# A graph layer and a state-space layer on one core: GpSimd's softplus spread over four slots, ScalarE's moved by one, one of two comparisons moved to GpSimd, and the first image's last edges moved into the layer-1 loop

## The chip, the core and the metric

The kernel runs on one core of one Trainium2 chip. The metric is the device time of one execution in microseconds (us). "Before" has a median of 14244.15 us over three runs (14243.77 to 14252.39).

The engines are named as the profile names them: PE is TensorE (PEld are its weight loads), DVE is VectorE, ACT is ScalarE, POOL is GpSimd, SP is the engine whose queue issues most DMAs.

## The reference

The input x has 16 images of 96 channels by 64 by 64 pixels, float32. Two layers are computed one after the other.

Layer 0 works on windows of 8x8 pixels. A 1x1 convolution gives 64 nodes a window; each node finds its 9 nearest nodes; an edge function is computed for every neighbour and the largest value is kept:

```
nodes = window_partition(affine(conv1x1(x, fc1_w, fc1_b), fc1_s, fc1_t), 8)
idx   = knn_idx(nodes, 9)                      # top 9 of the normalized distances
feat  = concat(x_i, x_j - x_i)                 # x_j = nodes[idx]
h     = max over the 9 of gelu(affine(feat @ ew.T + eb, es, et))
x1    = affine(conv1x1(window_reverse(h), fc2_w, fc2_b), fc2_s, fc2_t) + x
```

Layer 1 treats an image as a sequence of 4096 positions and runs two state-space blocks over it, each with 192 channels and 16 states:

```
delta = softplus(dt @ dt_w + dt_b);   dA = exp(delta * A);   dBx = delta * B * xc
h[l]  = dA[l] * h[l-1] + dBx[l]       # for each channel and state, along the sequence
y     = (sum over states of h * C + D * xc) * silu(z);   seq = seq + y @ out_w
```

Then follow a fusing 1x1 convolution with a pooled term, a normalization over the whole batch, and the sum with layer 1's input.

## The kernel before

**Work units.** Layer 0 works by strips of 8 pixel rows, 512 positions, 8 strips an image. `nearest(b, q)` (lines 281 to 353) loads a strip, projects it, computes distances and picks the 8 neighbours of each node other than itself; `edges(b, q)` (355 to 475) does the rest of layer 0 in two halves (`hf`). In a half, the neighbours' numbers come back by DMA as 16-bit integers, broadcast to 64 partitions (`idb`, 362). Each is compared with the partition's own number to make a one-hot matrix: `Abs(idb - node)` (370) and `Relu(1 - that)` (371), two ACT operations on 64x1024 elements, once for each of two pairs of windows (`oh0`, `oh1`). Two products `pv` (380, 381) are copied to SBUF by ACT (`vu`, 383). For each pair, three products `t` of one-hot and `vu` (400, 403) go through Gelu on ACT (408); DVE reduces them by maximum in later slots (780). The node's own term (`sa`, `sb`, 426 and 438) is added in the second half.

Layer 1 works by items: one image, one block, one strip, 16 x 2 x 8 = 256 items. `norm(n)` (504 to 525) normalizes the strip; `prelude(n)` (527 to 611) projects it, applies the short convolution and SiLU, and computes softplus; `tail(n)` (657 to 685) projects back and, in the second block, computes `po` and the copy `o`.

**The main loop** (729 to 795) runs over 256 items x 8 slots, p = 0 to 7, each slot for two of the 16 states. In a slot DVE does three products `db` (635) and three scans `hb` (776), with other small work between them; PE broadcasts the next slot's B into `bt` (630) and folds an earlier slot's result over the states (`folded`: `ya`, `yb`, 646 and 648); ACT computes three exponentials `da` for a slot two ahead (624); POOL copies the state (791) and multiplies `hb` by C (792).

**The order is written out by hand** (`manual_schedule`, 699): every engine takes its instructions in the order in which the program emits them. Beside the scan, the steps of `norm`, `nearest`, `edges` and `tail` (the list `going`) and then those of `prelude` (the list `preps`) are advanced by one `yield` in each slot, between the first and the second scan. In PE's queue a slot m thus reads: `bt` for slot m+1, the steps' products, the fold of slot m-1. `bt` has one PSUM buffer; the steps' products share a ring of two (`mm`), so that a product waits until the last but one has been read. The exponentials of a slot are emitted in the middle of the slot for p = 0, 2, 4, ahead of the steps, and otherwise at its end; a step that yields `TABLE` holds the latter back for that slot.

For the prediction, these places matter. `prelude(n+2)` starts at p = 4 of item n. In item n, the steps of p = 0 to 3 therefore are:

- p = 0: `pc` and its square (515, 517) of `norm(n+2)`; first `pv` and `vu`; `po` and `o` (679, 681) in the second block; and ACT's four softplus passes of `prelude(n+1)` (589 to 594).
- p = 1: `pvar` (520) and the two ACT passes `rs` on it (522, 523); `ss` and its copy (306, 307) in even items; second `pv` and `vu`; POOL's first two softplus passes (596, 597).
- p = 2: `hn` on POOL (525); the first pair's three `t` and Gelus, with a table load ahead of the first; POOL's last two passes (599, 600).
- p = 3: the second pair's `t` and Gelus; 16 DMAs that double `ln` and `s1` into `delta` and `u` (607, 609).

`edges` starts at p = 5 of odd items with `idb`, the comparisons are at p = 6, and the second half starts one item later. `nearest` starts in the same slots; its product `pf` and copy `y` fall on p = 7 of odd items.

**Before the loop** come the loads of the constants, all issued on SP's queue (98 to 221); `nearest(0, 0)` alone; eight calls of `drain` (704), each with `nearest(0, q+1)` and `edges(0, q)` side by side (the last with `edges(0, 7)` alone); then `norm` and `prelude` of items 0 and 1. **After the loop** a normalization pass reads everything back, adds and writes the result (801 to 822).

Of the kernel before, what the change touches and what calls it, by code (L numbers as in the profile page):

```python
# [10 lines left out]
F32 = mybir.dt.float32  # L11
U16 = mybir.dt.uint16
AF = mybir.ActivationFunctionType
ALU = mybir.AluOpType
# [6 lines left out]
def tile_conv_knn_mamba(ctx: ExitStack, tc: tile.TileContext, w: dict, out: bass.AP):  # L21
# [29 lines left out]
    CB = 64  # L51
    NB3 = D // CB
# [4 lines left out]
    const = ctx.enter_context(tc.tile_pool(name="const", bufs=1))  # L57
# [5 lines left out]
    make_identity(nc, ident)  # L63
    cmat = const.tile([C, C], F32, name="cmat")
    nc.vector.tensor_scalar(cmat, ident[:C, :C], -1.0 / C, None, ALU.add)
    minus_node = const.tile([NN, 1], F32, name="minus_node")
    nc.gpsimd.iota(minus_node, pattern=[[0, 1]], base=0, channel_multiplier=-1, allow_small_or_imprecise_dtypes=True)
# [37 lines left out]
    def compact(name, src):  # L105

        t = const.tile([128, 2], F32, name=name)
        src = src.rearrange("(p o) -> p o", o=1)
        nc.sync.dma_start(out=t[:, 0:1], in_=src[:128])
        for h in range(2):  # L110
            nc.sync.dma_start(out=t[h * CB : (h + 1) * CB, 1:2], in_=src[128:])
        return t

    def rows(name, src, n):


        t = const.tile([128, 3, n], F32, name=name)
        nc.vector.memset(t, 0.0)
        nc.sync.dma_start(out=t[:, 0, :], in_=src[:128])
        for h in range(2):  # L120
            nc.sync.dma_start(out=t[h * CB : (h + 1) * CB, 1 + h, :], in_=src[128:])
        return t

    fc1T = load("fc1T", [C, C], w["L0_conv_fc1_w"])
# [39 lines left out]
    for i in range(NHN):  # L164
        t = const.tile([128, HALO + Q], F32, name=f"hn{i}")
# [3 lines left out]
    for i in range(2):  # L169
        t = const.tile([128, Q], F32, name=f"dbl{i}")  # L170
# [4 lines left out]
    with tc.tile_pool(name="setup", bufs=2) as sp, tc.tile_pool(name="setup_ps", bufs=2, space=PSUM) as spp:  # L175
        for i in range(NL):


            iw = sp.tile([C, 2 * D], F32, tag="iw", name=f"in_w{i}")
            nc.sync.dma_start(out=iw, in_=w["L1_conv_in_w"][i])  # L180
            g = sp.tile([C, 1], F32, tag="g", name=f"g{i}")
            nc.sync.dma_start(out=g, in_=w["L1_conv_ln_g"][i].rearrange("(p o) -> p o", o=1))
            lb = sp.tile([C, C + 1], F32, tag="lb", name=f"lb{i}")
            nc.vector.memset(lb, 0.0)
            nc.sync.dma_start(out=lb[:, C : C + 1], in_=w["L1_conv_ln_b"][i].rearrange("(p o) -> p o", o=1))
# [12 lines left out]
            cw = sp.tile([C + 1, NT, D], F32, tag="cw", name=f"cw{i}")  # L198
            nc.sync.dma_start(
                out=cw.rearrange("p k d -> p (k d)"),  # L200
                in_=w["L1_conv_conv_w"][i].rearrange("k d -> (k d)").unsqueeze(0).to_broadcast([C + 1, NT * D]),
            )
# [10 lines left out]
            nc.sync.dma_start(out=dw[:R], in_=w["L1_conv_dt_w"][i])  # L213
            nc.sync.dma_start(out=dw[R + 2 * NS : R + 2 * NS + 1], in_=w["L1_conv_dt_b"][i].rearrange("(o d) -> o d", o=1))
            dt_w.append(dw)
            an = const.tile([128, NB3, NPR], F32, name=f"a{i}")
            for k in range(NB3):
                for h in range(2):
                    nc.sync.dma_start(
                        out=an[h * CB : (h + 1) * CB, k, :],  # L220
                        in_=w["L1_conv_A_log"][i].rearrange("(k c) (n h) -> h k c n", c=CB, h=2)[h, k],
                    )
# [20 lines left out]
    pr = main.enter_context(tc.tile_pool(name="ring", bufs=2))  # L243
# [15 lines left out]
    def half(h):  # L259
        return slice(h * CB, (h + 1) * CB)  # L260
# [94 lines left out]
    def edges(b, q):  # L355

        nm = f"{b}_{q}"
        y = nodes_of.pop((b, q))
        idx_d = chosen_of.pop((b, q))
        for hf in range(2):  # L360
            idb = pr.tile([NN, NP, NN * KO], U16, tag="idb", name=f"idb_{nm}_{hf}", bufs=1)
            nc.sync.dma_start(
                out=idb.rearrange("j w n -> j (w n)"),
                in_=idx_d.rearrange("(s p) i k -> s (p i k)", s=2)[hf : hf + 1].to_broadcast([NN, NP * NN * KO]),
            )
            yield
            for p in range(2):

                ohj = ohs[p][0:NN].rearrange("j w i k -> j w (i k)")
                nc.scalar.activation(ohj, idb[:, 2 * p : 2 * p + 2, :], AF.Abs, bias=minus_node)  # L370
                nc.scalar.activation(ohj, ohj, AF.Relu, bias=1.0, scale=-1.0)
            yield
            yield
            vus = []
            for p in range(2):

# [150 lines left out]
    def prelude(n):  # L527
# [57 lines left out]
        for v, cols in ((va, slice(0, Q)), (vb, slice(Q, Q + QH))):  # L585
            nc.scalar.activation(e[:, cols], v, AF.Abs)
            nc.scalar.activation(rl[:, cols], v, AF.Relu)
        yield
        nc.scalar.activation(e, e, AF.Exp, scale=-1.0)
        s1 = pr.tile([128, Q + QH], F32, tag="s1", name=f"s1_{nm}", bufs=1)  # L590
        nc.scalar.activation(s1, e, AF.Identity, bias=1.0)
# [2 lines left out]
        nc.scalar.activation(s1, s1, AF.Identity, bias=neg1)  # L594
        yield
        nc.gpsimd.tensor_tensor(e, e, s1, ALU.subtract)  # L596
        nc.gpsimd.tensor_tensor(ln, ln, e, ALU.add)
        yield
        nc.gpsimd.tensor_tensor(ln, ln, rl, ALU.add)
        nc.gpsimd.tensor_tensor(s1, ln, xc, ALU.mult)  # L600
        yield
        pairs = []
        for what, src in (("delta", ln), ("u", s1)):
            t = pr.tile([128, NB3, Q], F32, tag=what, name=f"{what}_{nm}")
            for h in range(2):
                for k in range(2):
                    nc.sync.dma_start(out=t[half(h), k, :], in_=src[half(k), :Q])
                for k in range(2):
                    nc.sync.dma_start(out=t[half(h), 2, bass.ts(k, QH)], in_=src[half(k), Q:])
            pairs.append(t)  # L610
        made[n] = (xc, z, dbl, c_d, *pairs)

    def chosen(n, p):

# [86 lines left out]

    drain(nearest(0, 0))
    for q in range(NQ):
        drain(*([nearest(0, q + 1)] if q + 1 < NQ else []), edges(0, q))
    for n in range(2):
        drain(norm(n))
        drain(prelude(n))
# [141 lines left out]
```

## Time and profile before

| what | value |
|---|---|
| median of three runs | 14244.15 us |
| the profiled execution | 14254.24 us, span 14252.5 us |
| first `db` of the loop | 485.9 us after the start of the span |
| last scan of the loop | 13970.8 us |
| busy in the span | DVE 12875.6 us (90%), PE 12467.5 (87%), ACT 10536.6 (74%), POOL 10043.0 (70%) |
| busy from 4000 to 6000 us | DVE 1887.76, PE 1824.15, ACT 1547.43, POOL 1483.67 us of 2000 |
| granted PE clock over the span, from 4000 to 6000 us | 0.951, 0.97 |

The profile tells for each group of instructions its line in the kernel, the engine, the operation, the tiles as out<-in, the shapes and the count; behind the first bar the busy time in us and the mean of one in ns; behind the second bar how long the engine stood idle just before them, with what ended that. The timeline gives each instruction's start and duration in us, and in brackets the idle time before it and its releaser. PE's instructions are pipelined, so that their durations overlap; starts are read there.

### The profile page before, as it was taken

How to read it: one execution, taken by the hardware profiler on the slowest of the kernel's cores; microseconds unless marked ns; L12 is line 12 of the kernel's file. 1: busy time of each engine (PE TensorE's matmuls, PEld its weight loads, DVE VectorE, ACT ScalarE, POOL GpSimd, SP SyncE). 2: the span in 40 equal slices, each digit the busy share in tenths (PEclk: the TensorE clock that was granted, in tenths of full speed). 3: DMA queues.
4: the chain of work that ended last, by engine and by line, in shares of the span. 5: the costliest groups of instructions: out<-in, count | busy, mean ns of one | idle time of the engine just before them, and what ended most of it. 6: DMA issues, size and time to landing. Idle time of an engine off the chain costs nothing. (4 is left out here: it accounts for less than half of the span.)

```text
span 14252.5 us, 162557 instructions
## 1 busy us (share of the span) xinstructions
PE 12467.5 (87%) x47944; PEld 4659.7 (33%) x47944; DVE 12875.6 (90%) x16893; ACT 10536.6 (74%) x15157; POOL 10043.0 (70%) x6151
## 2 busy tenths in 40 slices
PE   5799999999999999999999999999999999999871
PEld 2233333333333333333333333333333333333320
DVE  2699999999999999999999999999999999999984
ACT  4577777777777777777777777777777777777652
POOL 0477777777777777777777777777777777777771
PEclk8899999999999999999999999999999999999985
DMA  1233333333333333233333333333333333333227
GB/s 25 57 85 86 80 85 84 84 82 81 87 83 81 86 84 84 80 85 84 86 81 84 86 81 82 84 86 85 81 86 83 84 81 83 87 84 81 78 76 226
DMA packets 887149, 1206.23 MB, mean 85 GB/s; under 512 B 282272, under 2 KB 413742, under 8 KB 877040
## 3 DMA queue, kind: packets, MB, share of 16 engines
q1 hardware_dynamic: 882672, 1170.66, 31.1%
q10 hardware_dynamic: 3584, 25.17, 0.4%
q8 instruction: 377, 6.18, 0.2%
q14 instruction: 516, 4.23, 0.1%
HBM read 706.82 MB, written 85.72 MB: 56 GB/s over the span
## 5 line engine op out<-in xcount | busy, mean ns | idle before, releaser
L792 POOL TENSOR_TENSOR hb<-hb,ct 128x1536 f32<-128x1536 f32 x2048 | 7068.3, 3452 | 608.4 <-DVE hb L776 233.2
L776 DVE TENSOR_TENSOR_SCAN hb<-da,state,db 128x512 f32<-128x512 f32 x5376 | 6808.9, 1270 | 0.0
L635 DVE TENSOR_TENSOR db<-u,bt 128x512 f32<-128x512 f32 x6144 | 3988.9, 679 | 827.1 <-PE bt L630 827.1
L624 ACT ACTIVATE da<-delta,a 128x512 f32<-128x512 f32 x6144 | 3903.5, 716 | 38.5 <-DVE hb L776 32.5
L646 PE MATMUL ya<-hb,fold 128*64 128x512 f32 x8192 | 2324.1, 647 | 410.9 <-POOL hb L792 409.4
L630 PE MATMUL bt<-dbl,bsel 128*128 128x512 f32 x4096 | 2351.0, 656 | 101.0 <-DVE db L635 85.8
L408 ACT ACTIVATE g<-t,eb,es 128x512 f32<-128x512 f32 x1536 | 1178.3, 776 | 1098.9 <-PE t L400 660.2
L791 POOL COPY state<-hb 128x3 f32<-128x3 f32 x1792 | 336.2, 188 | 2219.9 <-DVE hb L776 2162.6
L648 PE MATMUL yb<-hb,fold 128*64 128x256 f32 x8192 | 1292.7, 395 | 0.0
L554 ACT ACTIVATE xc<-pj,conv_b 128x512 f32<-128x512 f32 (+1 forms) x512 | 297.1, 580 | 1058.0 <-PE pj L547 791.0
L648 PEld LDWEIGHTS yb<-hb,fold 128*64 128x64 f32 x8192 | 617.8, 144 | 1281.8 <-issue 1281.6
L400 PE MATMUL t<-oh,vu 128*128 128x512 f32 x2048 | 992.7, 607 | 31.8 <-ACT g L408 19.0
L646 PEld LDWEIGHTS ya<-hb,fold 128*64 128x64 f32 x8192 | 491.5, 142 | 1448.1 <-POOL hb L792 675.6
L630 PEld LDWEIGHTS bt<-dbl,bsel 128*128 128x128 f32 x4096 | 639.1, 193 | 959.9 <-issue 501.9
L542 PE MATMUL pj<-hn,conv_in 128*128 128x512 f32 x2048 | 929.1, 596 | 9.2 <-POOL hn L525 9.2
L776 DVE TENSOR_TENSOR_SCAN hb<-da,db 128x512 f32<-128x512 f32 x768 | 924.6, 1210 | 2.3 <-ACT da L624 2.3
L596 POOL TENSOR_TENSOR e<-e,s 128x768 f32<-128x768 f32 x256 | 464.9, 1816 | 626.3 <-ACT s L594 593.4
L403 PE MATMUL t<-oh,vu 128*64 128x512 f32 x2048 | 604.5, 671 | 341.0 <-ACT g L408 337.4
L380 PE MATMUL pv<-ewT,y 96*64 96x192 f32 x2048 | 475.4, 358 | 257.9 <-ACT rs L522 247.5
L370 ACT ACTIVATE oh<-idb,minus_node 64x1024 f32<-64x1024 uint16 x512 | 581.1, 1135 | 71.8 <-DMA idb<-idxd 71.7
L780 DVE TENSOR_REDUCE hqa<-g 128x64 f32<-128x512 f32 x960 | 633.3, 660 | 0.0
L400 PEld LDWEIGHTS t<-oh,vu 128*128 128x128 f32 x2048 | 394.5, 195 | 555.6 <-issue 440.5
(164 smaller groups left out, 16884.9 us busy)
## 6 DMA issues: line engine op xcount, KB each, us to landing
ct<-cd SPq DMA_DIRECT2D x4096, 128.0 KB
delta<-ln SPq DMA_DIRECT2D x1024, 128.0 KB
u<-s SPq DMA_DIRECT2D x1024, 128.0 KB
idb<-idxd SPq DMA_DIRECT2D x256, 256.0 KB
delta<-ln SPq DMA_DIRECT2D x1024, 64.0 KB
u<-s SPq DMA_DIRECT2D x1024, 64.0 KB
x<-in_x SPq DMA_DIRECT2D x128, 192.0 KB
rn<-r4d SPq DMA_DIRECT2D x128, 192.0 KB
```

The costliest lines, as they stand in the source:

```text
L400: nc.tensor.matmul(t, lhsT=vus[p][:, part, :128], rhs=ohw[part], start=True, stop=True)
L403: nc.tensor.matmul(t[half(h)], lhsT=vus[p][:, h, 128:], rhs=ohw[h], start=True, stop=True)
L408: nc.scalar.activation(g, t, AF.Gelu, bias=e_b[:, j : j + 1], scale=e_s[:, j : j + 1])
L542: nc.tensor.matmul(ps, lhsT=wt[:, t, :128], rhs=hn[:, off : off + Q], start=(t == 0), stop=(t == taps - 1))
L624: nc.scalar.activation(da, delta[:, c, :], AF.Exp, scale=a_neg[i][:, c, p : p + 1])
L630: nc.tensor.matmul(bt, lhsT=bsel[:, p, :], rhs=made[n][2], start=True, stop=True)
L635: nc.vector.tensor_tensor(db, made[n][5][:, c, :], bt, ALU.mult)
L646: nc.tensor.matmul(y[0][half(h)], lhsT=fold, rhs=hb[:, h, :], start=False, stop=(p == NPR - 1))
L648: nc.tensor.matmul(y[1][half(h)], lhsT=fold, rhs=hb[:, 2, bass.ts(h, QH)], start=False, stop=(p == NPR - 1))
L776: nc.vector.tensor_tensor_scan(hb[:, c, :], das[c], dbs[c], state[:, p, c : c + 1] if k else 0.0, ALU.mult, ALU.add)
L780: between.popleft()()
L792: nc.gpsimd.tensor_tensor(hb, hb, ct.unsqueeze(1).to_broadcast([128, NB3, Q]), ALU.mult)
```

## The change

1. Softplus: ACT's four passes are emitted one slot later (p = 1 instead of p = 0), after the steps in `going`, so behind the two passes `rs` and the copies of that slot. POOL's four passes stand at p = 2, 3, 4 and 5, one in each, instead of two at p = 1 and two at p = 2. The eight DMAs to `delta` follow at p = 5, the eight to `u` at p = 6, instead of all at p = 3.
2. Comparisons: for the second pair ACT does the same two passes at p = 6; for the first pair POOL does one `is_equal` with the partition's number at p = 7.
3. The first image: `drain` runs `edges(0, 0)` to `edges(0, 5)` only. `edges(0, 6)` is advanced by three steps before the loop and goes on in it; `edges(0, 7)` starts at item 1. The later strips start where they did.
4. Constants: the loads in `compact` and `rows`, and those of the block's weights, are issued on ACT's queue instead of SP's.

```diff
@@ edges
-            for p in range(2):
-
+            for p in (1, 0):
                 ohj = ohs[p][0:NN].rearrange("j w i k -> j w (i k)")
-                nc.scalar.activation(ohj, idb[:, 2 * p : 2 * p + 2, :], AF.Abs, bias=minus_node)
-                nc.scalar.activation(ohj, ohj, AF.Relu, bias=1.0, scale=-1.0)
-            yield
-            yield
+                numbers = idb[:, 2 * p : 2 * p + 2, :]
+                if p == 0:
+                    nc.gpsimd.tensor_scalar(ohj, numbers, node, None, ALU.is_equal)
+                else:
+                    nc.scalar.activation(ohj, numbers, AF.Abs, bias=minus_node)
+                    nc.scalar.activation(ohj, ohj, AF.Relu, bias=1.0, scale=-1.0)
+                yield
@@ prelude
             nc.scalar.activation(rl[:, cols], v, AF.Relu)
         yield
+        yield
         nc.scalar.activation(e, e, AF.Exp, scale=-1.0)
...
         nc.gpsimd.tensor_tensor(e, e, s1, ALU.subtract)
+        yield
         nc.gpsimd.tensor_tensor(ln, ln, e, ALU.add)
         yield
         nc.gpsimd.tensor_tensor(ln, ln, rl, ALU.add)
+        yield
+        delta = pr.tile([128, NB3, Q], F32, tag="delta", name=f"delta_{nm}")
+        doubled(delta, ln)
+        u = pr.tile([128, NB3, Q], F32, tag="u", name=f"u_{nm}")
         nc.gpsimd.tensor_tensor(s1, ln, xc, ALU.mult)
-        yield
...
+        made[n] = (xc, z, dbl, c_d, delta, u)
+        yield
+        doubled(u, s1)
+
+    def doubled(t, src):
+
+        for h in range(2):
+            for k in range(2):
+                nc.sync.dma_start(out=t[half(h), k, :], in_=src[half(k), :Q])
+            for k in range(2):
+                nc.sync.dma_start(out=t[half(h), 2, bass.ts(k, QH)], in_=src[half(k), Q:])
@@ before the loop
-        drain(*([nearest(0, q + 1)] if q + 1 < NQ else []), edges(0, q))
+        drain(*([nearest(0, q + 1)] if q + 1 < NQ else []), *([edges(0, q)] if q < NQ - 2 else []))
...
-    going, preps = [], []
+    going, preps = [edges(0, NQ - 2)], []
...
-    edge_row = NQ
+    edge_row = NQ - 1
+    for _ in range(3):
+        next(going[0])
@@ in the loop
-        if n > 1 and n % 2 == 1 and p == 5 and edge_row < NB * NQ:
+        if n % 2 == 1 and p == 5 and edge_row < NB * NQ:
@@ compact (the same in rows and for the block's weights)
-        nc.sync.dma_start(out=t[:, 0:1], in_=src[:128])
+        nc.scalar.dma_start(out=t[:, 0:1], in_=src[:128])
```

More of the change, by code (lines that the diff above doesn't have):

```diff
@@ L65, in tile_conv_knn_mamba @@
     nc.vector.tensor_scalar(cmat, ident[:C, :C], -1.0 / C, None, ALU.add)
+    node = const.tile([NN, 1], F32, name="node")
+    nc.gpsimd.iota(node, pattern=[[0, 1]], base=0, channel_multiplier=1, allow_small_or_imprecise_dtypes=True)
     minus_node = const.tile([NN, 1], F32, name="minus_node")
-    nc.gpsimd.iota(minus_node, pattern=[[0, 1]], base=0, channel_multiplier=-1, allow_small_or_imprecise_dtypes=True)
+    nc.vector.tensor_scalar(minus_node, node, -1.0, None, ALU.mult)
     neg1 = const.tile([128, 1], F32, name="neg1")
@@ L108, in compact @@
         src = src.rearrange("(p o) -> p o", o=1)
-        nc.sync.dma_start(out=t[:, 0:1], in_=src[:128])
+        nc.scalar.dma_start(out=t[:, 0:1], in_=src[:128])
         for h in range(2):
-            nc.sync.dma_start(out=t[h * CB : (h + 1) * CB, 1:2], in_=src[128:])
+            nc.scalar.dma_start(out=t[h * CB : (h + 1) * CB, 1:2], in_=src[128:])
         return t
@@ L118, in rows @@
         nc.vector.memset(t, 0.0)
-        nc.sync.dma_start(out=t[:, 0, :], in_=src[:128])
+        nc.scalar.dma_start(out=t[:, 0, :], in_=src[:128])
         for h in range(2):
-            nc.sync.dma_start(out=t[h * CB : (h + 1) * CB, 1 + h, :], in_=src[128:])
+            nc.scalar.dma_start(out=t[h * CB : (h + 1) * CB, 1 + h, :], in_=src[128:])
         return t
@@ L179, in tile_conv_knn_mamba @@
             iw = sp.tile([C, 2 * D], F32, tag="iw", name=f"in_w{i}")
-            nc.sync.dma_start(out=iw, in_=w["L1_conv_in_w"][i])
+            nc.scalar.dma_start(out=iw, in_=w["L1_conv_in_w"][i])
             g = sp.tile([C, 1], F32, tag="g", name=f"g{i}")
-            nc.sync.dma_start(out=g, in_=w["L1_conv_ln_g"][i].rearrange("(p o) -> p o", o=1))
+            nc.scalar.dma_start(out=g, in_=w["L1_conv_ln_g"][i].rearrange("(p o) -> p o", o=1))
             lb = sp.tile([C, C + 1], F32, tag="lb", name=f"lb{i}")
             nc.vector.memset(lb, 0.0)
-            nc.sync.dma_start(out=lb[:, C : C + 1], in_=w["L1_conv_ln_b"][i].rearrange("(p o) -> p o", o=1))
+            nc.scalar.dma_start(out=lb[:, C : C + 1], in_=w["L1_conv_ln_b"][i].rearrange("(p o) -> p o", o=1))
             gw = sp.tile([C, 2 * D], F32, tag="gw", name=f"gw{i}")
@@ L198, in tile_conv_knn_mamba @@
             cw = sp.tile([C + 1, NT, D], F32, tag="cw", name=f"cw{i}")
-            nc.sync.dma_start(
+            nc.scalar.dma_start(
                 out=cw.rearrange("p k d -> p (k d)"),
@@ L212, in tile_conv_knn_mamba @@
             nc.vector.memset(dw, 0.0)
-            nc.sync.dma_start(out=dw[:R], in_=w["L1_conv_dt_w"][i])
-            nc.sync.dma_start(out=dw[R + 2 * NS : R + 2 * NS + 1], in_=w["L1_conv_dt_b"][i].rearrange("(o d) -> o d", o=1))
+            nc.scalar.dma_start(out=dw[:R], in_=w["L1_conv_dt_w"][i])
+            nc.scalar.dma_start(out=dw[R + 2 * NS : R + 2 * NS + 1], in_=w["L1_conv_dt_b"][i].rearrange("(o d) -> o d", o=1))
             dt_w.append(dw)
@@ L218, in tile_conv_knn_mamba @@
                 for h in range(2):
-                    nc.sync.dma_start(
+                    nc.scalar.dma_start(
                         out=an[h * CB : (h + 1) * CB, k, :],
@@ L599, in prelude @@
         nc.gpsimd.tensor_tensor(ln, ln, rl, ALU.add)
+        yield
+        delta = pr.tile([128, NB3, Q], F32, tag="delta", name=f"delta_{nm}")
+        doubled(delta, ln)
+        u = pr.tile([128, NB3, Q], F32, tag="u", name=f"u_{nm}")
         nc.gpsimd.tensor_tensor(s1, ln, xc, ALU.mult)
+        made[n] = (xc, z, dbl, c_d, delta, u)
         yield
[L602 to L611, printed above, removed]
+        doubled(u, s1)
[5 more added lines that the diff above has]
+                nc.sync.dma_start(out=t[half(h), 2, bass.ts(k, QH)], in_=src[half(k), Q:])
     def chosen(n, p):
```

## The prediction

> **What bounds the kernel now.** I read the page's groups first, then the timeline of one pair of items in the second block (3017 to 3100 us), DVE, ACT and PE in turn.
>
> ```profile
> span 14252.5 us, 162557 instructions
> ...
> L776 DVE TENSOR_TENSOR_SCAN hb<-da,state,db 128x512 f32<-128x512 f32 x5376 | 6808.9, 1270 | 0.0
> L635 DVE TENSOR_TENSOR db<-u,bt 128x512 f32<-128x512 f32 x6144 | 3988.9, 679 | 827.1 <-PE bt L630 827.1
> ```
>
> DVE is the busiest engine, and in the loop it waits for one thing only: `bt`. Of the 827.1 us, 47.4 lie ahead of the loop's first `db` (485.92) and 14.4 in its first item (before 517.15); 765 are left, 3.0 an item, 6 a pair. The timeline shows where:
>
> ```profile
> 3041.60 0.70 DVE L635 TENSOR_TENSOR db<-u,bt 128x512 f32<-128x512 f32 x1 [3.76 <-PE bt L630]
> ...
> 3098.21 0.69 DVE L635 TENSOR_TENSOR db<-u,bt 128x512 f32<-128x512 f32 x1 [2.18 <-PE bt L630]
> ```
>
> The first is the `db` for slot 3 of an even item, the second that for slot 4 of an odd item. Why `bt` is late, in ACT's queue of the even item:
>
> ```profile
> 3028.43 0.59 ACT L517 ACTIVATE sqv<-pc 96x512 f32<-96x512 f32 x1 [2.82 <-PE pc L515]
> ...
> 3030.84 0.83 ACT L589 ACTIVATE e<-e 128x768 f32<-128x768 f32 x1
> ...
> 3034.34 0.67 ACT L522 ACTIVATE rs<-pvar,eps_t 96x512 f32<-96x512 f32 x1
> ...
> 3036.41 3.78 ACT L624 ACTIVATE da<-delta,a 128x512 f32<-128x512 f32 x6
> 3040.21 1.28 ACT L408 ACT_TABLE_LOAD   x1
> 3042.46 1.64 ACT L408 ACTIVATE g<-t,eb,es 128x512 f32<-128x512 f32 x2 [0.96 <-PE t L400]
> ```
>
> From the square at 3028.43 to the first Gelu at 3042.46 ACT hardly rests. PE hangs on it in two places: the second `pv` waits for `rs` (ring of two), which stands behind softplus, and the third `t` waits for the first Gelu. `bt` stands behind both in PE's queue:
>
> ```profile
> 3035.06 0.38 PE L380 MATMUL pv<-ewT,y 96*64 96x192 f32 x1 [2.27 <-ACT rs L522]
> ...
> 3093.10 1.17 PE L403 MATMUL t<-oh,vu 128*64 128x512 f32 x4 [3.34 <-ACT g L408]
> 3094.05 1.93 PE L646 MATMUL ya<-hb,fold 128*64 128x512 f32 x4
> ```
>
> The even item shows the first wait, the odd one the second. What follows a long wait runs slowly: that `ya` takes 1.93 us, otherwise 1.03 to 1.08. Two rows by stretch (length, busy times and counts of PE, PEld, DVE, ACT, POOL, then the granted clock) show it: 0.50 right after the wait, 1.00 afterwards.
>
> ```profile
> 3094.00:3097.40 3.40, 3.40 (x11) 1.24 (x8) 2.00 (x5) 0.78 (x1) 3.32 (x3) 0.50 0.11 10
> 3097.40:3100.80 3.40, 3.39 (x10) 0.96 (x8) 2.59 (x4) 1.55 (x2) 3.32 (x3) 1.00 0.70 166
> ```
>
> What starts the next round? After the `db` of 3046.75 DVE runs without a pause until slot 7's last scan ends at 3073.1; POOL's product then runs from 3073.55 to 3077.0; PE's fold (3077.07, after 0.28 us of waiting for that product), `pc` (3078.51) and ACT's square (3079.65) follow at once. So one item is: DVE from slot 4 to slot 7, then ACT from the square to Gelu, then PE from the third `t` to `bt`. PE's waits for POOL elsewhere (0.93 at 3050.45) are not on it.
>
> **POOL's passes, one a slot.** Four passes of 1.82 us stay. Two in a slot with product and state copy are 3.64 + 3.7 = 7.3 us, more than a slot (6.58 us mean, 13,485 us by 2048), and hold up that slot's product; one is 5.5. But the late product (3046.96) costs the 0.93 us above, in slot 4, which is off the round. Gain 0; at most 0.93 in even items, 110 us in 120.
>
> **ACT's passes, one slot later.** They still stand ahead of six `da`, the table load and the first Gelu, so the sum of ACT's work up to it stays. What changes is the waits.
>
> Even item, second block: the copy `o` ends at 3030.94; `pvar` starts at 3030.92 and takes 1.02, so `rs` starts at 3031.98, not 3034.34, after an idle 1.04 that softplus used to fill. Then, by starts in the rows: two `rs` 1.24, `ss` copy 0.46, `vu` 0.37 (34.1, a short wait for `pv` within), softplus 3.50 (37.6), six `da` 3.80 (41.4), table 1.29: Gelu at 3042.7. The 0.96 it waited for `t` is gone, the 1.04 is new: 0.24 later. PE gains: `pv` starts at 32.7, then `pv` 0.80, `ya` and `yb` 1.5 (odd item, full clock), fold 1.44, `bt` 1.1: 37.6, where DVE wants it at 37.8. **The 3.76 us stall goes.** The next thing is late instead: two `t` are done by 39.3, and PE waits for the first Gelu's end, 43.5, 4.2 us. The odd item, with such a wait, needs 5.11 us from the third `t` to `db` (3093.10 to 3098.21), half clock included; the even one needed 3.46 (3043.29 to 3046.75). So slot 4's `db` comes at 48.65 instead of 46.75: 1.9 later, and DVE, which wanted it at 43.0, stalls 5.6 there.
>
> Odd item, second block: `o` ends at 3082.12, `pvar` ends at 3083.16. ACT waits 1.04, everything to Gelu moves by it, and no wait goes: 1.04 later.
>
> First block (no `o`): even, softplus started at 2394.72 and `pvar` ends at 2396.22, 1.5 later; odd 2341.63 against 2343.12, 1.5. Gelu waited for nothing there. Pair: 3.0; half clock could add 1.65, which I leave to the range, because that wait was shorter.
>
> Both blocks: 1.9 + 1.04 = 2.9 and 1.5 + 1.5 = 3.0, so 3.0 us a pair. 120 strips run in the loop in both kernels, each in one pair: **+360 us**. Lower end 1.5 a pair (+180: no half clock, half of the new wait hidden), upper 3.8 (+456).
>
> A page of the Trainium skill speaks to the half clock: by "TensorE: Matmul & The Clock Gate", Part 1, the clock falls after an idle window of about 3.4 us. Here a wait of 2.27 us was enough (0.51 from 3035.9 to 3039.3). By the page the new 4.2 us wait would cover a whole window of a free-running grid only one time in four, a second-block pair would cost 1.7 in place of 2.9 and the sum of this part would be an estimated +280 us; the trace decides.
>
> **One comparison on POOL.** ACT loses 1.13 + 1.06 at p = 6, where it later waits for PE anyway (0.74 before `e` at 3073.96): nothing. POOL's `is_equal` on 64x1024 has no row. Above: two inputs of 96x512 take 1.27, 2.48 ns an element, 2.54 us. Below: select over 128 takes 0.28 and a copy of 3 takes 0.19, 0.72 ns an element, 0.93 us. At p = 7 of the even item POOL stood idle 1.99 us; only what exceeds it delays the product that the round runs through: 0 to 0.55 a pair, 66 us at most. I take 1.7 us (the middle), so nothing. The Trainium skill, "GPSIMD Engine Reference", 3.1, has 512 elements in 769 ns, an estimate of 1.54 us here, also hidden.
>
> **DMAs of `delta` and `u`.** Eight issues are 4.8 us of SP (0.6 each). For `u`, POOL's last pass ends some 5.5 us into p = 5; issued in p = 6, landing within 3.4 us (`idb`: 90.38 to 93.77) is 8.2 into p = 6; the `db` that needs it is 10.3 us in. `delta` has more room. The `ct` issues behind them are used two slots on. Cost 0; were it late, each us costs 256.
>
> **Ahead of the loop.** Strip 5's result is stored at 356.70, strip 7's at 437.83; `nearest` alone takes 25.7 (62.1 to 87.8). Removed: 81.1 - 25.7 = 55.4. The 12 halves left lose up to 2.1 us of ACT each: 25. Constants: SP issues until 62.1, 6.6 of it remain ahead of `x`; but ACT must issue the rest, 55 us, and wait for one load, before it can do `y`, at about 58 instead of 67.04: 9. Given back: two strips in the loop, 12 maxima of 0.57 and 2.3 us of other DVE work each, 18. Sum **-70 us** (-40 to -110).
>
> **Sum.** 14254.24 + 360 - 70 = 14544. The profiled execution stands 10 us above the median: 14530 us, 1.02 times the time before.
>
> **Rivals.**
> *ACT's new wait is hidden and the clock costs nothing new*: only the lead-in shows, 14254 - 70 - 10 = 14175 (14110 to 14250). For it: the 0.96 us wait for `t` that goes. Against it: the odd item has nothing that goes.
> *The stalls go and nothing takes their place* (the faster side): even items lose a stall of the mean, 3.0 us, 120 x 3.0 = 360; 14175 - 360 = 13815. Place: the third `t`. It decides if the first Gelu ends 3.46 us before 3043.0, so starts by 3038.7, 10.3 us after the square. For it: slots 1 and 2 do lose what held PE and POOL. Against: 14.0 us now, with softplus still ahead; without it 10.5.
> *POOL becomes the bound*: `is_equal` on 16-bit input at twice the bound, 5.1 us, exceeds the gap by 3.1 each pair: +370, 14900. No row speaks for it.
>
> **Chances.** Forecast 0.64, lead-in alone 0.17, stalls gone 0.12, POOL 0.07. About 0.2% is what a measurement of this kernel can tell from no change, 28 us. Faster: 0.12 of the lead-in case and all 0.12 of the stalls gone, 0.24. Within: 0.05 of the lead-in case and 0.02 of the forecast. Slower: 0.62 of the forecast and 0.07 of POOL, 0.69. The forecast's own range is 14350 to 14650. The range for 8 in 10 takes in the lead-in rival: 14050 to 14700.
>
> **What would show it.** Right: no stall before slot 3 in even items; stalls of 5 us and more before slot 4; `rs` waiting 1.0 to 1.5 us for `pvar`; PE waiting 4 us for the first Gelu; the first `db` 90 us earlier. Wrong: square to Gelu not longer than now (14.0 and 12.6 us), slot 4's stall under 3 us, or POOL waiting on its comparison.

## The result, and the profile after

After the change the kernel takes 14806.37 us (median of four runs, 14805.01 to 14809.24), before it 14246.74 (four runs, 14243.77 to 14252.39): a ratio of 1.0393 [1.0375, 1.0411], 560 us slower. The prediction said slower, 14530 us, and at most 14700. The direction was right and the size was not: the rise was forecast at 290 us and came to 560.

The page of the kernel after, the same groups as before and the new comparison:

```profile
span 14803.3 us, 161728 instructions
...
L790 DVE TENSOR_TENSOR_SCAN hb<-da,state,db 128x512 f32<-128x512 f32 x5376 | 6806.5, 1269 | 0.0
L647 DVE TENSOR_TENSOR db<-u,bt 128x512 f32<-128x512 f32 x6144 | 3984.4, 678 | 1443.7 <-PE bt L642 1443.7
...
L409 PE MATMUL t<-oh,vu 128*64 128x512 f32 x2048 | 732.8, 802 | 989.7 <-ACT g L414 987.0
...
L375 POOL TENSOR_SCALAR oh<-idb,node 64x1024 f32<-64x1024 uint16 x256 | 731.2, 2856 | 127.4 <-DMA idb<-idxd 127.4
```

The scans cost what they did. DVE's wait for `bt` is 1443.7 us where it was 827.1: 617 more, nearly all of the 638 us by which the loop grew, while its start moved forward by 86.6. PE's third `t` (L409 now) waited 337.4 us for Gelu before and 987.0 now; the row of before:

```profile
L403 PE MATMUL t<-oh,vu 128*64 128x512 f32 x2048 | 604.5, 671 | 341.0 <-ACT g L408 337.4
```

And the comparison, whose duration no row of before showed, takes 2856 ns.

DVE's timeline shows where the stall went; an even and an odd item of the second block:

```profile
3110.14 0.70 DVE L647 TENSOR_TENSOR db<-u,bt 128x512 f32<-128x512 f32 x1 [6.27 <-PE bt L642]
```
```profile
3164.74 0.70 DVE L647 TENSOR_TENSOR db<-u,bt 128x512 f32<-128x512 f32 x1 [5.32 <-PE bt L642]
```

Both are the `db` for slot 4. The stall before slot 3 of even items is gone in all of them. ACT's queue in the even item, and PE's wait in the same item:

```profile
3088.75 0.59 ACT L523 ACTIVATE sqv<-pc 96x512 f32<-96x512 f32 x1 [2.97 <-PE pc L521]
...
3092.30 0.68 ACT L528 ACTIVATE rs<-pvar,eps_t 96x512 f32<-96x512 f32 x1 [1.04 <-PE pvar L526]
...
3094.39 0.84 ACT L596 ACTIVATE e<-e 128x768 f32<-128x768 f32 x1
...
3101.64 1.28 ACT L414 ACT_TABLE_LOAD   x1
3102.93 1.45 ACT L414 ACTIVATE g<-t,eb,es 128x512 f32<-128x512 f32 x2
```
```profile
3103.76 1.98 PE L409 MATMUL t<-oh,vu 128*64 128x512 f32 x4 [4.14 <-ACT g L414]
3105.53 1.92 PE L658 MATMUL ya<-hb,fold 128*64 128x512 f32 x4
3107.23 1.07 PE L660 MATMUL yb<-hb,fold 128*64 128x256 f32 x4
3108.23 1.87 PE L642 MATMUL bt<-dbl,bsel 128*128 128x512 f32 x2
```

From square to Gelu it is 14.18 us (14.03 before); `rs` waits 1.04 for `pvar`, and PE 4.14 for the first Gelu. Then everything up to `bt` runs at half speed: `bt` in 1.87 us instead of 1.1. The granted clock, by stretch (columns as in the prediction), falls to 0.50 right after the wait:

```profile
3099.60:3103.00 3.40, 0.02 (x1) 0.00 (x0) 3.40 (x5) 3.37 (x6) 3.32 (x4) 0.99 0.50 148
3103.60:3107.00 3.40, 3.24 (x8) 1.01 (x10) 0.27 (x1) 1.56 (x3) 3.16 (x5) 0.50 0.07 28
3107.00:3110.40 3.40, 3.40 (x10) 1.29 (x7) 0.26 (x1) 0.00 (x0) 1.82 (x2) 0.59 0.19 51
3110.40:3113.80 3.40, 3.39 (x14) 1.12 (x14) 3.40 (x5) 2.38 (x4) 1.70 (x2) 1.00 0.44 138
```

The other new thing is on POOL, at the end of the same item:

```profile
3131.23 3.45 POOL L806 TENSOR_TENSOR hb<-hb,ct 128x1536 f32<-128x1536 f32 x1
3134.66 2.86 POOL L375 TENSOR_SCALAR oh<-idb,node 64x1024 f32<-64x1024 uint16 x1
3137.47 0.18 POOL L805 COPY state<-hb 128x3 f32<-128x3 f32 x1
3137.73 3.45 POOL L806 TENSOR_TENSOR hb<-hb,ct 128x1536 f32<-128x1536 f32 x1
```
```profile
3141.23 1.08 PE L658 MATMUL ya<-hb,fold 128*64 128x512 f32 x4 [2.20 <-POOL hb L806]
```

POOL goes from comparison to copy to product without a rest, and PE waits 2.20 us for the product from which the odd item's round starts. In the odd items of before that wait was 0.73 to 0.77 on average.

To weigh every run by the same measure, I cut an item into three stretches, taken from the trace: **X** from slot 4's first `db` to the square, **Y** from the square to the first Gelu, **Z** from the first Gelu to the next item's slot 4 `db`. The table gives them in us for a pair of items (mean over items 20 to 229, both blocks), with the lead-in (first `db`) and the 14 items at the end, which have no `edges`.

| kernel | median us | lead-in | last 14 | X | Y | Z | pair |
|---|---|---|---|---|---|---|---|
| before | 14246.74 | 485.9 | 703.9 | 69.9 | 25.2 | 10.5 | 105.6 |
| after | 14806.37 | 399.4 | 665.1 | 70.1 | 27.7 | 13.3 | 111.0 |
| e1, comparisons back | 14601.86 | 418.2 | 657.9 | 69.3 | 27.1 | 12.9 | 109.3 |
| e2, ACT's softplus back | 14190.98 | 393.7 | 656.1 | 70.2 | 25.7 | 10.4 | 106.2 |
| e3, POOL's passes back | 14805.72 | 398.3 | 678.8 | 70.0 | 27.6 | 13.3 | 110.9 |
| e4, lead-in only | 14194.64 | 422.2 | 708.1 | 70.0 | 25.3 | 10.2 | 105.5 |
| e5, lead-in and spread | 14072.87 | 419.0 | 664.7 | 69.3 | 25.4 | 10.1 | 104.8 |
| e7, clock kept up | 14602.61 | 400.0 | 660.4 | 70.3 | 28.4 | 10.8 | 109.5 |
| e8, one half on POOL | 14004.03 | 406.6 | 664.6 | 69.0 | 25.1 | 10.2 | 104.4 |
| e12, clock kept up longer | 14203.03 | 418.9 | 656.0 | 69.3 | 27.1 | 9.6 | 106.0 |
| e6, softplus behind Gelu | 14582.14 | 421.1 | 692.3 | 77.6 | 20.9 | 10.2 | 108.7 |
| e9, `u` earlier | 14429.47 | 419.4 | 650.4 | 77.0 | 20.2 | 10.6 | 107.8 |
| e10, `idb` first | 13924.74 | 416.2 | 653.1 | 73.0 | 20.2 | 10.6 | 103.7 |
| e11, same, one half on POOL | 13904.64 | 405.8 | 652.0 | 72.8 | 20.2 | 10.6 | 103.6 |

Before and after differ by 2.5 us a pair in Y and 2.8 in Z. The kernel before was measured again beside each group of runs, on different chips of the same kind: its medians were 14243 to 14260, so a difference between runs of two groups is good to some 15 us.

### The profile page after: what moved, and what is told of

Same layout as the page of the kernel before. It is cut to its first block, busy times and chain, and to the rows that moved or that the text cites. A ratio compares the mean times of both kernels' runs of the same rounds, so it can differ in the third digit from the quotient of the medians.

```text
span 14803.3 us, 161728 instructions
## 1 busy us (share of the span) xinstructions
PE 12696.9 (86%) x47944; PEld 4737.0 (32%) x47944; DVE 12863.1 (87%) x16894; ACT 10017.3 (68%) x14645; POOL 10757.5 (73%) x6407
## 5 line engine op out<-in xcount | busy, mean ns | idle before, releaser
L647 DVE TENSOR_TENSOR db<-u,bt 128x512 f32<-128x512 f32 x6144 | 3984.4, 678 | 1443.7 <-PE bt L642 1443.7
L658 PE MATMUL ya<-hb,fold 128*64 128x512 f32 x8192 | 2393.4, 665 | 383.6 <-POOL hb L806 363.9
L642 PE MATMUL bt<-dbl,bsel 128*128 128x512 f32 x4096 | 2405.7, 670 | 132.3 <-DVE db L647 104.3
L409 PE MATMUL t<-oh,vu 128*64 128x512 f32 x2048 | 732.8, 802 | 989.7 <-ACT g L414 987.0
L660 PE MATMUL yb<-hb,fold 128*64 128x256 f32 x8192 | 1339.9, 408 | 0.0
L658 PEld LDWEIGHTS ya<-hb,fold 128*64 128x64 f32 x8192 | 523.4, 146 | 1446.3 <-issue 660.5
L375 POOL TENSOR_SCALAR oh<-idb,node 64x1024 f32<-64x1024 uint16 x256 | 731.2, 2856 | 127.4 <-DMA idb<-idxd 127.4
L523 ACT ACTIVATE sqv<-pc 96x512 f32<-96x512 f32 x256 | 151.9, 593 | 775.1 <-PE pc L521 775.1
L409 PEld LDWEIGHTS t<-oh,vu 128*64 128x64 f32 x2048 | 119.2, 160 | 1429.9 <-ACT g L414 1429.9
```

The costliest lines, as they stand in the source:

```text
L375: nc.gpsimd.tensor_scalar(ohj, numbers, node, None, ALU.is_equal)
L409: nc.tensor.matmul(t[half(h)], lhsT=vus[p][:, h, 128:], rhs=ohw[h], start=True, stop=True)
L642: nc.tensor.matmul(bt, lhsT=bsel[:, p, :], rhs=made[n][2], start=True, stop=True)
L647: nc.vector.tensor_tensor(db, made[n][5][:, c, :], bt, ALU.mult)
L658: nc.tensor.matmul(y[0][half(h)], lhsT=fold, rhs=hb[:, h, :], start=False, stop=(p == NPR - 1))
L660: nc.tensor.matmul(y[1][half(h)], lhsT=fold, rhs=hb[:, 2, bass.ts(h, QH)], start=False, stop=(p == NPR - 1))
```

## The experiments

Theory A holds that ScalarE's later softplus, with the half clock behind its new wait, and the comparison's overrun on GpSimd carry the loss. Its rivals: the comparison mainly (theory B), and GpSimd's spread passes or their late DMAs (theory C).

### One part undone at a time

**e1, both comparisons on ScalarE again.**

```
-            for p in (1, 0):
+            for p in range(2):
...
-                    nc.gpsimd.tensor_scalar(ohj, numbers, node, None, ALU.is_equal)
```

> The changed kernel with both comparisons on ScalarE at p = 6 again; all else as changed. Theory A (the loop's +638 us over the lead-in's gain are ScalarE's later softplus with the half clock behind its new wait, some 450 to 490 us, and the comparison on GpSimd, which takes 2.86 us where 1.99 us were free and so holds up the product at the head of odd items, some 150 to 190 us): 14615 to 14655 us; PE's ya no longer waits 2.1 us for hb at p = 0 of odd items. Theory B (the comparison is the main cost): 14400 us or less. Theory C (GpSimd's spread passes or the late DMAs of delta and u are the main cost): within 30 us of 14806.

14601.86 us, ratio to before 1.0248 [1.0231, 1.0265]: 204 less than after, a little past A's 150 to 190. The lead-in is 19 us longer, so the loop gains 223. Theory B falls.

**e2, ScalarE's softplus in slot 0 again.**

```
         yield
-        yield
         nc.scalar.activation(e, e, AF.Exp, scale=-1.0)
...
+        yield
         yield
         nc.gpsimd.tensor_tensor(e, e, s1, ALU.subtract)
```

> The changed kernel with ScalarE's softplus passes in slot 0 again; GpSimd's stay one a slot at p = 2 to 5, and the comparison stays on GpSimd. Theory A: the stall goes back from before slot 4 to before slot 3 and the half clock behind it goes; 450 to 490 us less, 14315 to 14355. Theory B: 14700 or more. Theory C: 14700 or more.

14190.98 us, 0.9957 [0.9940, 0.9973]: 615 less, much more than the 450 to 490 expected. So e1 and e2 together take away 820 us, where the change lost 560: the parts are not additive, and something else in the change must gain.

**e3, GpSimd's passes two and two, DMAs together.**

```
         nc.gpsimd.tensor_tensor(e, e, s1, ALU.subtract)
-        yield
         nc.gpsimd.tensor_tensor(ln, ln, e, ALU.add)
         yield
         nc.gpsimd.tensor_tensor(ln, ln, rl, ALU.add)
+        nc.gpsimd.tensor_tensor(s1, ln, xc, ALU.mult)
         yield
...
-        nc.gpsimd.tensor_tensor(s1, ln, xc, ALU.mult)
...
-        yield
         doubled(u, s1)
```

> The changed kernel with GpSimd's softplus passes two and two at p = 2 and p = 3, and the DMAs of delta and u together at p = 4. Theory A: nothing, 14776 to 14836, or up to 60 us slower, as two passes in a slot hold up that slot's product. Theory C (the spread passes or the later DMAs cost): 14600 or less.

14805.72 us, 1.0392 [1.0374, 1.0409]: no difference. Theory C falls: neither the spread passes nor the later DMAs cost anything in the changed kernel.

### One part alone

**e4, the kernel before with the lead-in parts** (constants on ScalarE's queue; `edges(0, 6)` and `edges(0, 7)` in the loop).

```
-        drain(*([nearest(0, q + 1)] if q + 1 < NQ else []), edges(0, q))
+        drain(*([nearest(0, q + 1)] if q + 1 < NQ else []), *([edges(0, q)] if q < NQ - 2 else []))
```

> The kernel before with the two lead-in parts alone: constants on ScalarE's queue, the first image's last two strips in the loop. Theory A: first db 86 us earlier, 10 to 25 us given back in the first four items: 14170 to 14190. Rival (of the changed kernel's 26 us more in items 0 to 3, all belongs to the two strips and more follows from them): 14200 or more.

14194.64 us, 0.9962 [0.9948, 0.9976]: 55 less. The first `db` is 63.7 us earlier (not 86: the other 19 to 23 us of the changed kernel come from the comparisons, as e1 shows), and items 0 to 3 take 17.7 us more.

**e5, the same with GpSimd's passes one a slot** (p = 1 to 4), softplus on ScalarE in slot 0. Against e4:

```
         nc.gpsimd.tensor_tensor(e, e, s1, ALU.subtract)
+        yield
         nc.gpsimd.tensor_tensor(ln, ln, e, ALU.add)
...
-        nc.gpsimd.tensor_tensor(s1, ln, xc, ALU.mult)
         yield
...
+        nc.gpsimd.tensor_tensor(s1, ln, xc, ALU.mult)
...
+        yield
         doubled(u, s1)
```

> The lead-in parts as in the run before (14194.64 us) and GpSimd's passes one a slot at p = 1 to 4 with the later DMAs of delta and u; ScalarE's softplus in slot 0, both comparisons on ScalarE. Theory A as amended by the four runs (with softplus in slot 0 the spread passes are worth something: the 14 items without edges took 708 us with the passes two and two and 656 us with them spread): 14195 - 52 and up to 120 less in the items with edges, 14020 to 14145 us. The prediction's own step (spread worth nothing): 14180 to 14210. Its distance from the changed kernel with the comparisons back (14601.86) is then the price of ScalarE's move alone; the prediction had 360 for it.

14072.87 us, 0.9871 [0.9855, 0.9888]: the spread alone gains 122, of which 43 lie in the last 14 items (708.1 to 664.7) and 0.7 a pair in X. From e5 to e1 ScalarE's softplus moves by a slot, and GpSimd's passes and their DMAs follow it by one: +529, with X unchanged, Y +1.7 and Z +2.8 a pair.

### The half clock by itself

**e7: PE is kept at work in its wait.** Five matmuls that add zeros to `yb` stand ahead of the third `t`.

```
+                    if p == 0 and part == 2 and spare:
+                        for _ in range(5):
+                            nc.tensor.matmul(
+                                spare[0], lhsT=ident, rhs=nought.to_broadcast([128, QH]), start=False, stop=False
+                            )
```

> The changed kernel with five matmuls of 128x256 more between the second and the third t of the first pair in each half, which add zeros to yb, so that PE works where it waits 4 us for the first Gelu; nothing else is changed. Theory A with the half clock (the wait puts PE on half clock, and what follows it up to bt takes about 2 us more in an item): from first Gelu to slot 4's db 4 to 4.8 us in place of 6.2 to 7.6; 14250 to 14450 us. Rival (that stretch is long for another reason, the clock costs nothing): 14790 us or more, slower by what the added matmuls take.

14602.61 us, 1.0236 [1.0219, 1.0253]. A gain of 204, less than expected. Z falls by 2.5 us a pair, but the five matmuls fill only half of the wait (PE still stands 2.0 us in even items and more in odd ones), and Y rises by 0.7, most of it in odd items of the second block (14.3 to 15.4 us), for a reason that is not traced.

**e12: nine such matmuls**, on e1, so without the comparison's overrun. Against e7:

```
-                        for _ in range(5):
+                        for _ in range(9):
```

> The changed kernel with the comparisons back on ScalarE (14601.86 us), with nine added matmuls of 128x256 between the second and the third t of the first pair, which add zeros to yb. Five of them shortened PE's wait for the first Gelu from 4.1 to about 2.0 us, so nine, 0.42 us each, should leave 0.4. Theory A (half clock behind that wait is what the prediction sized too small): third t to bt runs at full clock in every item, first Gelu to slot 4's db takes 4.0 to 4.6 us in place of 5.8 to 7.2; 3.5 to 4.5 us a pair, 14070 to 14190 us, about where softplus in slot 0 stands (14072.87). Rival (half clock is worth no more than the 2.5 us a pair that five matmuls took off this stretch): 14280 to 14330. Rival (the added matmuls end behind the Gelu and delay the third t as much as they save): 14400 or more.

14203.03 us, 0.9968 [0.9956, 0.9981]: 399 less than e1, with more work on PE. The page and a row of 2000 us of the loop (columns as before):

```profile
L416 PE MATMUL t<-oh,vu 128*64 128x512 f32 x2048 | 553.9, 619 | 61.2 <-ACT g L421 58.7
```
```profile
4000.00:6000.00 2000.00, 1909.14 (x7726) 799.70 (x7722) 1875.96 (x2469) 1541.68 (x2224) 1479.56 (x904) 1.00 0.32 83
```

The granted clock is 1.00, where the same row of e1 has 0.95 (0.94 in the kernel after):

```profile
4000.00:6000.00 2000.00, 1777.13 (x6838) 665.13 (x6836) 1821.44 (x2401) 1495.11 (x2157) 1438.28 (x882) 0.95 0.31 81
```

X and Y are those of e1 to a tenth; Z alone falls, by 3.3 us a pair. ScalarE's chain is as late as in e1, and yet 399 us are gone, where its move cost 529. Not all of the 399 belong to the move: Z is now shorter than in e5 (10.1) and before (10.5), where PE already waited for the first Gelu in odd items (2.1 to 3.0 us in e5). The half clock is shown, and the rival that puts it at 2.5 us a pair falls.

14203 lies 13 us above the range, because the other rival holds in one odd item of each image (14 of the 210, 16 items apart). There PE waits for the first Gelu already at the second `t`, the nine matmuls run behind it and delay the third:

```profile
5810.94 1.65 PE L413 MATMUL t<-oh,vu 128*128 128x512 f32 x2 [4.43 <-ACT g L421]
5812.38 5.28 PE L408 MATMUL yb<-nought,ident 128*128 128x256 f32 x18
```

Z is 10.7 to 12.2 us in these items and 4.3 to 4.5 in all others; that is some 100 us of the kernel.

### Where the comparison costs

**e8, GpSimd compares in the first half of a strip only**, at p = 7 of odd items; otherwise e5. The edit against the changed kernel's lines:

```
-                if p == 0:
+                if p == 0 and hf == 0:
+                    yield
                     nc.gpsimd.tensor_scalar(ohj, numbers, node, None, ALU.is_equal)
...
+            if hf:
                 yield
+            yield
```

> The run with the lead-in parts and GpSimd's passes one a slot (14072.87 us), and GpSimd does one comparison in the first half of each strip alone, which falls on p = 7 of odd items, where GpSimd stood idle 3.8 us; in the second half (p = 7 of even items, idle 1.5 us, comparison 2.86 us) ScalarE keeps both. With both halves on GpSimd the same loop took 14190.98 us, 118 more though the lead-in was 25 us shorter. Theory A (the 143 us are the overrun of the even item's gap, which delays the product that odd items start from): all of it goes and half of the lead-in's gain stays, 14040 to 14075 us. Rival (the comparison costs because GpSimd or the product t gets the one-hot matrix later, in either half): half of the 143 us stays, 14120 to 14150.

14004.03 us, 0.9832 [0.9816, 0.9849]. With no half on GpSimd (e5) it was 14073, with both (e2) 14191. The half in odd items gains 69, the half in even items costs 187. In e2 GpSimd's softplus passes also stand one slot later than in e5 and e8; e1, where they stand so as well, has the X of e5, so X does not grow by that.

It's the place and not the work, but not in the way that was expected: the gap of 3.8 us lies ahead of GpSimd's product of p = 7, and the comparison runs behind that product, in odd and even items alike, where GpSimd otherwise stands idle 2.0 to 2.2 us. The end of an odd item in e5 and in e8:

```profile
3573.02 0.19 POOL L802 COPY state<-hb 128x3 f32<-128x3 f32 x1 [3.71 <-DVE hb L787]
3573.28 3.45 POOL L803 TENSOR_TENSOR hb<-hb,ct 128x1536 f32<-128x1536 f32 x1
3578.92 0.19 POOL L802 COPY state<-hb 128x3 f32<-128x3 f32 x1 [2.19 <-DVE hb L787]
```
```profile
3547.10 3.44 POOL L808 TENSOR_TENSOR hb<-hb,ct 128x1536 f32<-128x1536 f32 x1
3550.52 2.87 POOL L376 TENSOR_SCALAR oh<-idb,node 64x1024 f32<-64x1024 uint16 x1
3553.33 0.19 POOL L807 COPY state<-hb 128x3 f32<-128x3 f32 x1
```

So it overruns in both kinds of item. The next product starts 2.67 to 2.82 us into slot 0 instead of 2.15 to 2.17 (means in e8, e2 and after against e5 and e1). At the head of an even item the square nevertheless comes 0.3 us earlier; at the head of an odd item, where the square hangs on that product, it comes 1.05 us later.

The traces also show what follows. In odd items PE's `ya` typically waits 2.1 us for the product in the kernel after, in e2 and in e7, and 0.9 in e1, e5 and e8 (medians). Behind the longer wait `pvar` took over 1.2 us, up to 1.9, instead of 1.02 in 15 of 105 odd items of the kernel after, in 12 of e2 and 24 of e7, and in none of e1, e5, e8 and before. So the overrun costs delay in X, and now and then the clock in Y as well: in the 15 items of the kernel after Y is 15.0 to 17.0 us on average (first and second block), in its other odd items 13.2 to 13.5.

### Taking softplus out of the chain

If the stretch from square to Gelu bounds the loop, it helps to put ScalarE's softplus behind it. **e6** is e4 with those passes at p = 3, behind both pairs of Gelu, and GpSimd's at p = 4 and 5.

```
             nc.scalar.activation(rl[:, cols], v, AF.Relu)
         yield
+        yield
+        yield
+        yield
         nc.scalar.activation(e, e, AF.Exp, scale=-1.0)
```

> The lead-in parts alone, and ScalarE's four softplus passes at p = 3 behind both pairs of Gelu; GpSimd's passes two at p = 4 and two at p = 5, delta's DMAs at p = 5, u's at p = 6. Theory A (the work that stands on ScalarE between the square and the first Gelu sets the length of an item): the 3.5 us of softplus leave that stretch, 1.0 us of waiting for pvar come in, the stalls before slots 3 and 4 shrink from 5.5 us a pair to under 2; 13600 to 13800 us. Rival D (ScalarE's six exponentials, the table load or PE's own queue hold the Gelu anyway): 14100 to 14200. Rival E (delta or u comes too late for the next item): over 14200, with a new stall at slot 0.

14582.14 us, 1.0231 [1.0214, 1.0248]: rival E. Y does fall, by 4.4 us a pair, and the stalls before slots 3 and 4 are nearly gone; but X grows by 7.6. DVE's timeline has the reason, and the page its sum:

```profile
3100.22 0.70 DVE L645 TENSOR_TENSOR db<-u,bt 128x512 f32<-128x512 f32 x1 [5.30 <-DMA u<-s]
```
```profile
L645 DVE TENSOR_TENSOR db<-u,bt 128x512 f32<-128x512 f32 x6144 | 3983.6, 678 | 958.7 <-DMA u<-s 726.0
```

Slot 0 waits for `u`, whose eight DMAs stand on SP's queue behind the eight of `delta`.

**e9, three of GpSimd's passes at p = 4, `delta` at p = 4, `u` at p = 5**, and the first third of each tile first. Against e6, without the order of the DMAs:

```
         nc.gpsimd.tensor_tensor(ln, ln, e, ALU.add)
-        yield
         nc.gpsimd.tensor_tensor(ln, ln, rl, ALU.add)
-        nc.gpsimd.tensor_tensor(s1, ln, xc, ALU.mult)
         delta = pr.tile([128, NB3, Q], F32, tag="delta", name=f"delta_{nm}")
         doubled(delta, ln)
+        yield
+        nc.gpsimd.tensor_tensor(s1, ln, xc, ALU.mult)
...
-        yield
         doubled(u, s1)
```

> The run with ScalarE's softplus behind both pairs of Gelu (14582.14 us), with GpSimd's passes three at p = 4 and one at p = 5 in place of two and two, delta's DMAs at p = 4, u's at p = 5, and in both the DMAs that fill the first third of the tile first. In that run DVE stalled 3.7 us (even) and 2.2 us (odd) before slot 0 for u's DMA, 5.9 us a pair, and the stalls before slots 3 and 4 were 0.1 and 0.6 us. Theory A (with u in time, nothing else is late, so that ScalarE's stretch from the square to the first Gelu is what bounds the loop before): 5 to 5.9 us a pair go, 13870 to 13980 us, faster than every kernel so far. Rival F (three passes in slot 4 hold up GpSimd's product and the fold, or another wait takes the place of u's): 14150 or more.

14429.47 us, 1.0136 [1.0119, 1.0153]: rival F. `u` is in time, and another wait takes its place. ACT's and DVE's timelines of one odd item and the next even one:

```profile
3127.79 1.15 ACT L374 ACTIVATE oh<-idb,minus_node 64x1024 f32<-64x1024 uint16 x1 [4.60 <-DMA idb<-idxd]
```
```profile
3139.59 0.75 DVE L473 SCALAR_TENSOR_TENSOR x<-pf,fc_b,x 96x512 f32<-96x512 f32 x1 [4.96 <-PE pf L464]
```

The load of `idb` is issued in slot 5 behind `delta`'s DMAs, which make SP wait for GpSimd. ACT waits 1085.3 us for `idb` in e9, 71.3 in e6.

**e10, `delta`'s DMAs at p = 5, behind `idb`'s load.** Against e9:

```
-        delta = pr.tile([128, NB3, Q], F32, tag="delta", name=f"delta_{nm}")
-        doubled(delta, ln)
         yield
+        delta = pr.tile([128, NB3, Q], F32, tag="delta", name=f"delta_{nm}")
+        doubled(delta, ln)
         nc.gpsimd.tensor_tensor(s1, ln, xc, ALU.mult)
```

> The run before (14429.47 us) with delta's DMAs issued at p = 5, behind idb's load and ahead of u's, in place of p = 4, where SP stood at delta until GpSimd's third pass had ended and idb went out behind it: ScalarE's comparisons then waited 3.6 to 4.6 us for idb, PE's pf for ScalarE, and DVE 4.96 us for pf in slot 0 of even items; the stall before slot 0 was already gone (0.35 and 0.2 us). Theory A (this wait is all that took the place of u's): slot 0 of even items falls from 10.2 to 6.7 us, slot 6 from 8.1 to 6.4, slot 6 of odd items from 8.5 to 7.4; 5 to 6.3 us a pair, 13680 to 13840 us. Rival F (another wait comes in its place; the stretch from the square to the first Gelu was only one of several bounds of like size): 14050 or more.

13924.74 us, 0.9761 [0.9745, 0.9777], 505 less than e9. It is faster than before by 2.4%, but short of the 13680 to 13840 expected: ACT's wait for `idb` is 69.4 us now and slot 0 of even items fell from 10.5 to 7.4 us (means), but slot 6 hardly (8.3 to 7.8 us in even items, 6.4 expected, and 8.5 in odd ones as before). Behind slot 6 of even items DVE still waits 1.3 us for `bt`; what makes slot 6 of odd items long is not traced.

```profile
L645 DVE TENSOR_TENSOR db<-u,bt 128x512 f32<-128x512 f32 x6144 | 3995.3, 681 | 350.5 <-PE bt L640 350.3
```

**e11, e10 with one comparison on GpSimd in odd items** (the edit of e8).

> The run with idb first, and GpSimd does one comparison in the first half of each strip, on p = 7 of odd items. Theory A (the gap there takes the 2.86 us whole): 10 to 70 us less than the run with idb first, of which 12 lie ahead of the loop, as the same step gave 69 us with softplus in slot 0. Rival (with the passes now at p = 4 and 5 the gap is no longer there): not less, or more.

13904.64 us, 0.9749 [0.9733, 0.9766]: 20 less, 10 of it in the lead-in. This is the fastest version found.

## Why the prediction was right in direction and wrong in size

- **What bounds the loop: right.** DVE waits for `bt` and hardly for anything else; e10 shortens the stretch Y by 5 us a pair, and DVE's wait for `bt` in the loop falls from 780 us (before) to 304. X gives back 3 us of it, more than the 1.3 us of waiting named above.
- **Where the stalls go: right.** None before slot 3 of even items; before slot 4 4.9 to 5.5 us on average in the four kinds of item (both blocks, even and odd); `rs` waits 364.1 us in 255 items, 1.4 each (1.0 to 1.5 forecast); PE waits 4.14 us for the first Gelu (4 forecast).
- **Lead-in: right.** Forecast 55 and 9 us earlier and 18 given back; e4 shows 63.7 and 17.7. For the comparisons there 25 were forecast and e1 shows 19. First `db`: 86.6 us earlier, 90 forecast.
- **DMAs of `delta` and `u`: right**, nothing (e3). In e6, where GpSimd's third pass ends a slot later and `delta`'s DMAs push `u`'s back, the stall for `u` is 726 us: the room was real and not large.
- **Spread passes: nothing forecast; nothing in the changed kernel** (e3), but 122 us when alone (e5). "Gain 0" was argued from the late product being off the round; 0.7 us a pair in X and 3.1 us in each of the last 14 items say otherwise. In the changed kernel, where the comparison runs on GpSimd too, X is back at 70.1; in e1, without it, 69.3.
- **The comparison: wrong, the step that failed.** "I take 1.7 us (the middle), so nothing." It takes 2.86 us, above the upper bound of 2.54, which came from a row with two inputs; 16-bit input was named only in a rival. Nor was the overrun's price the overrun: 2.86 less 1.99 are 0.87 us a pair, 104 us by the prediction's own rule, while the loop lost 223 (e1). By stretches, e1 to after, that is 0.7 us a pair in X (the late product), 0.6 in Y and 0.4 in Z. The items with a slow `pvar` account for some 0.5 in Y; where the rest comes from is open. The rival with the comparison had the mechanism and the total near (14900) from a wrong duration (5.1 us), at a chance of 0.07.
- **ScalarE's passes one slot later: near in Y, mis-sized in Z.** The forecast was 2.1 us a pair up to the Gelu and 0.8 behind it; e5 to e1 shows 1.7 and 2.8. The step that failed here is "half clock could add 1.65, which I leave to the range, because that wait was shorter", for the first block: PE's wait there came to 4.1 us in even and odd items alike (e1; in e5 0.2 and 2.1), and Z grew by 1.7 and 1.8 us where nothing was forecast. That the sum of lead-in, spread and move was nevertheless near (e1 407 above e4, 360 forecast) is luck: the spread's unforeseen gain of 122 us covered most of the 169 by which the move cost more than forecast.

The Trainium skill, "TensorE: Matmul & The Clock Gate", Part 1, ties the half clock to an idle window of about 3.4 us on a free-running grid. In this case's runs a wait of 4.1 us was followed by 0.50, and waits of 2.1 us by a slow `pvar` in some items and not in others (15 of 105); a wait of 0.9 us never. The clock records of all fourteen traces agree with the grid: the granted clock is 1.00 or 0.50 and changes only on a grid of 3.413 us. They disagree with the idle window: in the loop the clock fell after every stretch of this grid at 1.00 of which PE's matmuls filled less than 0.40, and after none of which they filled more than 0.56. So a wait of 2.1 us is enough when it lies within one stretch.

## What to carry to other kernels

When an engine's chain gets a new wait in it, ask what the engine that waits with it will do afterwards: here the stretch with PE's lost clock (Z) grew by 2.8 us a pair and the one with ScalarE's own delay (Y) by 1.7. A gap in an engine's time is only cover for work that surely fits it, and what an overrun costs depends on what hangs on the next instruction: the same 2.86 us in the same gap of some 2 us gained 69 us ahead of even items and cost 187 ahead of odd ones. And moving work out of the bounding chain shows the next bound only, often a transfer queued behind another: it took three steps (e6, e9, e10) until the gain was there.

## What the runs showed of the hardware

- GpSimd's `is_equal` of a 64x1024 16-bit tile with a number per partition takes 2.856 us, 2.79 ns for each of a partition's 1024 elements, more than its two-input float passes (2.48). The estimate of 1.54 us from the Trainium skill, "GPSIMD Engine Reference", 3.1, was too low by 1.3 us.
- Matmuls that only add zeros keep the clock: nine of 128x256 in the wait raise the granted clock from 0.95 (e1) to 1.00 (e12) and take 399 us off the kernel, though PE does more work.
- A DMA whose data are not ready holds up the ones behind it on SP's queue: in e9, with `idb`'s load behind `delta`'s DMAs, ACT waited 1085.3 us for `idb`, in e10, with the load ahead of them, 69.4, and the kernel was 505 us faster.
- The granted clock fell to 0.50 without a whole idle stretch of the 3.413 us grid: always when PE's matmuls filled under 0.40 of one, never when they filled over 0.56.
